# Order of TensorE's work in the attention rounds, and where the recurrence's units stand in it

## The chip, the core and the metric

The kernel runs on one core of a Trainium2 chip. Its engines work side by side, each through its own queue in order: TensorE (PE, with its weight loads as PEld), VectorE (DVE), ScalarE (ACT), GpSimd (POOL), and SyncE (SP), which here only issues transfers. The metric is the device time of one execution in microseconds (us). Everything is computed in fp32.

## What is computed

Four sequences of 1024 tokens with 1024 channels are normalized. An attention layer with 16 query heads and 4 key/value heads of 64 channels, a window of 512 keys and 4 sink keys, makes `s`. A second branch takes the last token of each sequence through a recurrence of four steps, gates with it, normalizes again and makes `g`. The output is `x + s * g`.

```python
mask = (j <= i) & (j >= i - (WINDOW - 1)) | (j < SINK)      # and causal for the first rows
att = softmax(where(mask, q @ k.T / sqrt(HS), -inf))
y = att @ v;  s = y @ Wo.T

thought = x_norm[:, -1, :] @ agg_w + agg_b
for _ in range(4):
    t = layer_norm(thought, pn_gamma, pn_beta)
    t = gelu(t @ d1_w + d1_b)          # 1024 -> 4096
    thought = thought + (t @ d2_w + d2_b)   # 4096 -> 1024
broadcast = thought @ bc_w + bc_b
g = silu(layer_norm(x + sigmoid(x @ gate_w + gate_b) * broadcast))
```

The recurrence works on four rows only. Its weights are read 1 MB at a time: 32 such transfers for d1 and d2, and again in each of the four steps.

## The kernel before

The kernel has three parts. The first makes keys, values, queries and gates (to about 970 us in the profile). The second is attention, with the recurrence between its instructions (to about 1889 us). The third multiplies with `Wo` and writes the output. The change touches the second alone.

Attention runs in 64 rounds, p = 0 to 63 (the loop at L1158). A round has two `Step`s of one pair of query tiles: `far`, a tile with a whole window (tiles 4 to 7 of a sequence), and `near`, a tile of the first half (tiles 0 to 3). A step covers one query tile, one of two key halves `m` and one of two row pairs `rp`, so four rounds belong to a pair of tiles. `n_near`, called n in this text, is the number of key tiles of the near step: 1 for four rounds, then 2, 3, 4, and the same again for each of the four sequences.

The steps' methods, with what each gives to which engine:

- `scores` (L257): TensorE multiplies queries and keys (L277, tiles `S`), VectorE moves the own keys into place (L282), takes the row maximum while it reads the scores (L299, `nm`), and ACT makes the exponentials with their sums (L304). There is a single buffer `S`, of four PSUM banks, for all scores, so scores can start only when the maxima of the scores before them have read it.
- `normalized` (L309): VectorE divides by the sums (L311, L315).
- `turned(k)` (L317): four transposes on TensorE (L322) turn the probabilities of key tile k into a PSUM tile `t`; ACT copies it to SBUF as `pT` (L326). For k = 0 of a far step VectorE also makes `lead` from it (L332).
- `turned_sinks` (L338): the same for the four sink keys, eight matmuls in the 128*32 shape (L344) and ACT's copy `sT` (L349). The tiles `t` and those of the sinks share two PSUM buffers, used in turn.
- `values(k)` (L359): TensorE multiplies `pT` of key tile k with the values (L354) into one tile `y`; `values_apart` (L366) adds the sinks (L371) and `lead`.
- `stored` (L378): VectorE copies `y` out (L384), and POOL's queue stores it (L389).

TensorE's order is written out by hand: the loop is under `manual_schedule` for that engine alone. For all other engines a planner sets the order from the program's order and what it takes to be ready. A round works on the transposes and values of its own steps, and on the scores of the next round's (`far_next`, `near_next`): far scores in two halves, near scores in one.

The recurrence is a generator, `ffn` (L953), that yields after each small unit of work. A stream unit (L977, matmuls at L986) loads 1 MB of weights into one of four buffers and multiplies it, eight matmuls in the 128*32 shape with 512 columns. The last unit of a stream copies the sums to SBUF (L992). The next unit turns them with four transposes (L1040) and adds them up on VectorE. Other units take mean and variance over the 1024 channels (L1060), from which VectorE and POOL make the next step's columns `t_cols` (L1096). The last unit of the first multiplication ends with ACT's gelu (L1107). `filler(slot)` (L1148) stands at three places of a round. It runs as many units as are due at that place, so that all 172 are done by round 62. In the profile a slot holds one unit or none.

Of the kernel before, what the change touches and what calls it, by code (L numbers as in the profile page):

```python
# [44 lines left out]
def recurrent_block_kernel(  # L45
# [356 lines left out]
    def steps_of(tiles, m, rp):  # L402
        return [Step(i, m, rp) for i in tiles]
# [17 lines left out]
    with ExitStack() as a:  # L421
# [434 lines left out]
        with tc.manual_schedule():  # L856
# [4 lines left out]
            for at, (kind, pair) in enumerate(passes):  # L861
                end = at + 1 == len(passes)
                after = None if end else passes[at + 1]
                todo, sums = {}, {}
# [32 lines left out]
                for k, i in enumerate(OUTER):  # L897
# [18 lines left out]
                    if end and k == 3:  # L916
# [9 lines left out]
                        far, near = steps_of(*order[0])  # L926
# [18 lines left out]
    with ExitStack() as a:  # L945
# [7 lines left out]
        def ffn():  # L953
# [23 lines left out]
            def streams(blocks, lhs, name):  # L977

                ps, sums = ps_f.tile([P, WIDE], F32, tag="F", name=f"{name}_ps"), None
                for u, (src, parts) in enumerate(blocks):
                    w = ws.tile([P, 4, WIDE], F32, tag="stream", name=f"{name}_w{u}")
                    nc.sync.dma_start(w, src)
                    for j, (k, moving) in enumerate(parts):
                        nc.tensor.matmul(  # L986
                            ps[j * QUAD : (j + 1) * QUAD, :], lhs[:, k, :], moving(w),
                            start=(u == 0), stop=(u == len(blocks) - 1),
                        )
                    if u == len(blocks) - 1:  # L990
                        sums = px.tile([P, WIDE], F32, tag="wide", name=f"{name}_sb", bufs=1)
                        nc.vector.tensor_copy(sums, ps)  # L992
                    yield sums
# [49 lines left out]
            def add_halves(dst, tr, base):  # L1043

                d4 = dst.rearrange("p (o k) b -> p o k b", o=2)
                b4 = base.rearrange("p (o k) b -> p o k b", o=2)
                nc.vector.tensor_tensor(d4, tr[:, 0:2, :, :B], b4, ALU.add)
                nc.vector.tensor_tensor(d4, tr[:, 2:4, :, :B], d4, ALU.add)
# [19 lines left out]
            def spread(v):  # L1068
                return v.unsqueeze(1).to_broadcast([P, DT, B])
# [8 lines left out]
            base = px.tile([P, DT, B], F32, tag="small", name="base_agg", bufs=4)  # L1078
            nc.vector.tensor_copy(base, along(biases["agg_b"]))
            for sums in streams(wide_blocks(agg_w, 0), t, "agg"):  # L1080
                yield
            add_halves(th, turned_rows(sums, "agg"), base)
            yield

            for s in range(K_STEPS):
                mean = over_d(th, f"mean{s}")
                d = px.tile([P, DT, B], F32, tag="small", name=f"d{s}", bufs=4)
                nc.vector.tensor_tensor(d, th, spread(mean), ALU.subtract)
                sq = px.tile([P, DT, B], F32, tag="small", name=f"sq{s}", bufs=4)
                nc.vector.tensor_mul(sq, d, d)  # L1090
                yield
                var = over_d(sq, f"var{s}")
                r = rstd_of(px, var, P, B, EPS_FFN, f"trs{s}")
                nc.vector.tensor_tensor(d, d, spread(r), ALU.mult)
                nc.vector.tensor_tensor(d, d, along(biases["pn_gamma"]), ALU.mult)
                nc.vector.tensor_tensor(t[:, :, :B], d, along(biases["pn_beta"]), ALU.add)  # L1096
                base = px.tile([P, DT, B], F32, tag="small", name=f"base{s}", bufs=4)
                nc.vector.tensor_tensor(base, th, along(biases["d2_b"]), ALU.add)
                yield
                bias = along_h(biases["d1_b"])  # L1100
                for g in range(H // D):
                    for sums in streams(wide_blocks(d1_w, g), t, f"d1_{s}_{g}"):
                        yield
                    at = slice(g * DT, (g + 1) * DT)
                    add_halves(hid[:, at, :B], turned_rows(sums, f"d1_{s}_{g}"), bias[:, at, :])
                    if g == H // D - 1:
                        nc.scalar.activation(hid[:, :, :B], hid[:, :, :B], AF.Gelu)  # L1107
                    yield
                th = px.tile([P, DT, B], F32, tag="th", name=f"th{s + 1}", bufs=2)
                for o in range(2):  # L1110
                    for sums in streams(deep_blocks(d2_w, o), hid, f"d2_{s}_{o}"):
                        yield
                    at = slice(o * 4, o * 4 + 4)
                    add_quarters(th[:, at, :], turned_rows(sums, f"d2_{s}_{o}"), base[:, at, :])
                    yield

            nc.vector.tensor_copy(t[:, :, :B], th)
            for sums in streams(wide_blocks(bc_w, 0), t, "bc"):
                yield
            ps = ps_f.tile([P, WIDE], F32, tag="F", name="bc_rows_ps")  # L1120
            nc.tensor.matmul(
                ps[: 2 * B, :], sel.rearrange("p b o -> p (b o)"), sums, start=True, stop=True
# [5 lines left out]
        per_half = DT // 2 + 1  # L1128
        FFN_UNITS = 3 + 2 * per_half + K_STEPS * (2 + (H // D) * per_half + 2 * (HT // 4 + 1))

        SLOTS = 3
        ffn_gen, ffn_done, ffn_steps = ffn(), 0, len(order) - 2

        def load_y(n, row):
# [13 lines left out]
        def filler(slot):  # L1148
            nonlocal ffn_done
            due = FFN_UNITS * (p * SLOTS + slot + 1) // (ffn_steps * SLOTS)  # L1150
            while ffn_done < min(due, FFN_UNITS + 1):
                next(ffn_gen, None)
                ffn_done += 1

        with tc.manual_schedule(engines={mybir.EngineType.PE}):
            for p in range(len(order)):  # L1158
                pair, within = divmod(p, per_pair)
                if within == 0:  # L1160
                    b, t = divmod(pair, TT // 2)
                    i = PAIRED[pair][0]
                    own = i % TT
                    leads[i] = px.tile([P, KVD], F32, tag="leads", name=f"leads{i}", bufs=2)
                    nc.vector.tensor_tensor(
                        leads[i], vs[b][:, own - WINDOW // P, :], vs[b][:, own, :], ALU.subtract
                    )
                    if pair + 1 < len(PAIRED):
                        for i in PAIRED[pair + 1]:
                            load_q(i)  # L1170
                    if t == 1 and b + 1 < B:
                        load_kv(b + 1)


                if 0 <= p - 2 * DT < 2 * DT:
                    c, g = divmod(p - 2 * DT, 2)
                    m, r = divmod(c, GROUP)
                    h = (2 * m + g) * GROUP + r
                    tc.keep_in_program_order(
                        nc.sync.dma_start(  # L1180
                            wo_sb[g * HS : (g + 1) * HS, c, :],
                            wo[h // 4, h % 2 * HS : (h % 2 + 1) * HS,
                               h // 2 % 2 * D : (h // 2 % 2 + 1) * D],
                        )
                    )
                if p > 4 * DT:
                    for dst, minuend, subtrahend in islice(wo_parts, 1):
                        tc.keep_in_program_order(
                            nc.vector.tensor_tensor(dst, minuend, subtrahend, ALU.subtract)
                        )  # L1190
                if p == ffn_steps:
                    for _ in ffn_gen:
                        pass
                    for row in range(2):
                        load_y(0, row)
                more = p + 1 < len(order)
                n_near = len(near.keys)
                far.turned(0)
                far.turned_sinks()
                if more:  # L1200
                    far_next, near_next = steps_of(*order[p + 1])
                    far_next.scores((0,))
                for k in (1, 2):
                    far.turned(k)
                filler(0)
                for k in range(3):
                    far.values(k)
                far.turned(3)
                if more:
                    far_next.normalized((0,))  # L1210
                    far_next.scores((1,))
                for k in range(min(2, n_near)):
                    near.turned(k)
                filler(1)
                far.values(3)
                far.values_apart()
                far.stored()
                for k in range(2, n_near):
                    near.turned(k)
                if more:  # L1220
                    far_next.normalized((1,))
                    near_next.scores(both)
                for k in range(n_near):
                    near.values(k)
                if more:
                    near_next.normalized(both)
                near.stored()
                filler(2)
                if more:
                    far, near = far_next, near_next  # L1230

# [275 lines left out]
```

## Time and profile before

| | |
|---|---|
| three timed runs | 2283.7, 2284.26, 2285.59 us (median 2284.26) |
| the profiled execution, its own time | 2284.38 us |
| its span, first to last instruction | 2282.7 us |
| granted TensorE clock, mean | 0.997 |
| score matmuls L277, busy | 259.7 us in 1536 |
| transposes L322, busy | 245.4 us in 1664 |
| values L354, busy | 221.9 us in 1664 |
| copies `pT` L326 on ACT, busy and mean | 229.9 us, 584 ns |
| exponentials L304 on ACT, busy | 324.6 us |

How to read it: a span in the profile is the time from the first to the last instruction. Each engine has a busy time, and groups of instructions are listed by line with the time of one and the idle time of the engine just before them, with what ended that idle time. Matmuls overlap one another in the array, so the busy time of one matmul is longer than the distance to the next; distances between starts tell more. A row of the timeline gives the start in us from the beginning of the span, the time the merged instructions cover, engine, line, operation, what is written and read, the shape, and how many instructions were merged; in brackets stands the idle time of the engine ahead of it and what ended it. ACT has, behind each exponential, a short instruction that reads its sum.

### The profile page before, as it was taken

Reading aid. Unit: us, or ns where it says so; the run is one execution under the profiler, and the core shown is the slowest. Engines: PE = TensorE matmul, PEld = TensorE weight load, DVE = VectorE, ACT = ScalarE, POOL = GpSimd, SP = SyncE. Lnnn points to the kernel's source line nnn. Section 1 sums busy time; section 2 is a strip of 40 time slices with the busy share of each in tenths; the row PEclk is TensorE's granted clock in tenths of the full one; section 3 lists DMA queues with packets and bytes.
Section 4 is the critical chain, followed back from the end, with each engine's and each line's share of the span. In section 5 each row is a group of like instructions: output and inputs, shape, how many; then the busy total and the mean of one; then the engine's idle time right before and its main releaser. Section 6 shows DMA issues by size and latency. Waiting matters only on the chain.

```text
span 2282.7 us, 34177 instructions
## 1 busy us (share of the span) xinstructions
PE 2225.9 (98%) x12614; PEld 1470.9 (64%) x12614; DVE 1735.6 (76%) x3821; ACT 854.5 (37%) x1968; POOL 393.9 (17%) x542
## 2 busy tenths in 40 slices
PE   7899999999999999999999999999999999999999
PEld 6778888888888888855555555555555554444444
DVE  6968688888868788877777777777777776777776
ACT  2121111112100000166665666666656663333332
POOL 3233225425411101310000000100000001111111
PEclk9999999999999999999999999999999999999999
DMA  8695333424533432586667776666566536675653
GB/s 270 233 337 212 107 111 107 147 99 174 215 137 112 160 104 99 163 279 206 192 209 235 229 231 208 210 215 209 169 215 226 190 103 212 179 206 168 171 161 92
DMA packets 214655, 416.60 MB, mean 183 GB/s; under 512 B 13284, under 2 KB 97332, under 8 KB 209368
## 3 DMA queue, kind: packets, MB, share of 16 engines
q1 hardware_dynamic: 170920, 266.12, 36.6%
q0 software_dynamic: 28288, 91.41, 12.9%
q10 hardware_dynamic: 15280, 56.89, 6.8%
q8 instruction: 99, 1.62, 0.3%
q14 instruction: 68, 0.56, 0.1%
HBM read 309.22 MB, written 121.93 MB: 189 GB/s over the span
## 4 chain that ended last, share of the span: by engine, by line
PE 72%; issue 13%; DVE 9%; POOL 3%; DMA 2%; ACT 1%; SPq 0%; POOLq 0%; ACTq 0%; DVEq 0%
PE u L1345 16%; PE u_q L789 13%; PE u_g L789 11%; PE S L277 7%; PE yp L354 7%; PE t L322 7%; PE d_ps L986 4%; PE u L573 3%; DVE t_g L805 2%; DVE st_a L117 1%; DVE f L742 1%; PE yp L371 1%; DVE wq L474 1%; PE xtp L487 1%; ACT pr L304 1%
## 5 line engine op out<-in xcount | busy, mean ns | idle before, releaser
L304 ACT ACTIVATE pr<-pr,nm 128x516 f32<-128x516 f32 (+4 forms) x512 | 324.6, 636 | 154.3 <-DVE nm L299 153.3
L299 DVE CUSTOM_DVE_ANT_0 pr<-S,near_mask 128x516 f32<-128x516 f32 (+4 forms) x512 | 278.3, 589 | 37.7 <-PE S L277 33.3
L326 ACT COPY pT<-t 128x512 f32<-128x512 f32 x416 | 229.9, 584 | 203.5 <-PE t L322 199.2
L277 PE MATMUL S<-kT,qT 64*128 64x512 f32 (+4 forms) x1536 | 259.7, 456 | 2.2 <-DVE nm L299 1.8
L322 PE MATMUL t<-ident,pr 128*128 128x128 f32 x1664 | 245.4, 282 | 7.3 <-ACT pT L326 5.4
L322 PEld LDWEIGHTS t<-ident,pr 128*128 128x128 f32 x1664 | 177.5, 141 | 103.1 <-issue 67.8
L354 PE MATMUL yp<-pT,v 128*64 128x256 f32 x1664 | 221.9, 391 | 0.5 <-DVE y L384 0.4
L277 PEld LDWEIGHTS S<-kT,qT 64*128 64x128 f32 x1536 | 129.6, 186 | 116.8 <-issue 95.5
L789 PE MATMUL u_g<-wg,f 128*128 128x256 f32 x864 | 197.4, 381 | 6.3 <-DVE f L742 6.3
L315 DVE TENSOR_SCALAR pr<-pr,ri 128x516 f32<-128x516 f32 (+4 forms) x512 | 198.6, 435 | 6.1
L789 PE MATMUL u_q<-f,wq_again 128*128 128x256 f32 x896 | 203.1, 379 | 0.0
L354 PEld LDWEIGHTS yp<-pT,v 128*64 128x64 f32 x1664 | 102.2, 136 | 144.3 <-issue 63.6
L789 PEld LDWEIGHTS u_q<-f,wq_again 128*128 128x128 f32 x896 | 169.8, 190 | 24.0 <-DVE f L742 0.9
L789 PEld LDWEIGHTS u_g<-wg,f 128*128 128x128 f32 x864 | 162.8, 190 | 34.0 <-DVE f L742 11.1
L1345 PE MATMUL u<-wo_sb,y 128*128 128x512 f32 x384 | 170.1, 592 | 1.1 <-DVE y L384 1.1
L389 POOL DMA_DIRECT2D y_dram<-y x64 | 36.1, 564 | 751.6 <-DVE y L384 634.4
L311 DVE RECIPROCAL ri<-s 128x2 f32<-128x2 f32 (+1 forms) x192 | 32.8, 171 | 137.3 <-ACT pr L304 136.8
L1345 PEld LDWEIGHTS u<-wo_sb,y 128*128 128x128 f32 x384 | 72.9, 190 | 92.9 <-issue 91.4
L805 DVE TENSOR_TENSOR t_q<-u_q,t_q 128x512 f32<-128x512 f32 x128 | 88.1, 689 | 54.9 <-PE u_q L789 39.3
L805 DVE TENSOR_TENSOR t_g<-u_g,t_g 128x512 f32<-128x512 f32 x128 | 87.9, 686 | 41.2 <-PE u_g L789 36.5
L835 ACT COPY t_q<-u_q 128x512 f32<-128x512 f32 x28 | 16.4, 584 | 273.4 <-PE u_q L789 273.4
L1345 PE MATMUL u<-wo_t,s 128*128 128x512 f32 x256 | 112.5, 592 | 0.0
(262 smaller groups left out, 3591.4 us busy)
## 6 DMA issues: line engine op xcount, KB each, us to landing
d_w<-in_d_w_dram SPq DMA_DIRECT2D x128, 1024.0 KB, 5.7
xT<-xT_dram SPq DMA_DIRECT2D x24, 1024.0 KB, 5.5
xn<-in_x_dram ACTq DMA_DIRECT2D x34, 512.0 KB, 5.1
x<-in_x_dram SPq DMA_DIRECT2D x64, 256.0 KB, 4.6
xT_dram<-xT POOLq DMA_DIRECT2D x32, 512.0 KB, 6.6
qT<-q_dram SPq DMA_DIRECT2D x32, 512.0 KB, 5.3
y_dram<-y POOLq DMA_DIRECT2D x64, 256.0 KB, 3.9
y<-y_dram SPq DMA_DIRECT2D x32, 512.0 KB, 4.7
```

The source lines that it names most:

```text
L277: nc.tensor.matmul(S[:, dst, g, at_s], qTs[self.i][half[g], at + r, :], k, start=True, stop=True,)
L299: nc.vector.tensor_tensor_reduce(out=low, in0=S[:, src, g, :cols], in1=self.mask, scale=-1.0 / HS**0.5, scalar=-NEG, op0=ALU.add, op1=ALU.min,
L304: nc.scalar.activation(low, low, AF.Exp, bias=nm, scale=-1.0, accum_out=self.sums[:, r, g : g + 1],)
L315: nc.vector.tensor_scalar(at, at, rinv[:, r, g : g + 1], None, ALU.mult)
L322: nc.tensor.transpose(ps[:, g, r, :], self.pr[g][:, r, k * P : (k + 1) * P], ident)
L326: nc.scalar.copy(self.pT[k], ps.rearrange("p g r q -> p g (r q)"))
L354: nc.tensor.matmul(self.y[g * HS : (g + 1) * HS, :], v[:, cols], pT[:, g, :], start=first, stop=last,)
L573: nc.tensor.matmul(bank, left[n][i].rearrange("p a (k q) -> p a k q", k=2)[:, c // 2, c % 2, j * P : (j + 1) * P], kv7[i][:, c, :], start= ...
L789: nc.tensor.matmul(bank[:, t * QD : (t + 1) * QD], stationary[:, at : at + P], moving[:, c * QD : (c + 1) * QD], start=(first and c == 0 a ...
L805: nc.vector.tensor_add(dst, in0, in1)
L986: nc.tensor.matmul(ps[j * QUAD : (j + 1) * QUAD, :], lhs[:, k, :], moving(w), start=(u == 0), stop=(u == len(blocks) - 1),)
L1345: nc.tensor.matmul(bank, left[n][i][:, c, j * P : (j + 1) * P], wo7[i][:, c, :], start=(first and c == 0), stop=(c == KH - 1), skip_group_ ...
```

## The change

Five things are changed, all in the attention loop and the generator that fills it.

- The first two transposes of the far step stand together at the start of the round, and the sinks' follow behind slot 0 and not directly behind the first transposes.
- Values come two key tiles at a time, two groups behind their transposes: tiles 0 and 1 behind the next far scores, and tiles 2 and 3 behind the near step's first transposes.
- The third and fourth transposes of the far step stand together, behind the first values.
- The recurrence has two places in a round and not three: slot 0 behind the first two transposes; slot 1 ahead of the second far scores, or, where the near step has one key tile only, at the end of the round. `SLOTS` is 2, so about 1.4 units are due at each place.
- `filler` goes on to a further due unit only if the unit before gave a true value. A stream unit gives one unless it is the last of its stream. All other units give none, and so end the slot; what is due then waits for the next slot.

```diff
-                yield
+                yield sums is None
...
-        SLOTS = 3
+        SLOTS = 2
...
             while ffn_done < min(due, FFN_UNITS + 1):
-                next(ffn_gen, None)
                 ffn_done += 1
+                if not next(ffn_gen, None):
+
+                    break
...
-                far.turned(0)
+                for k in (0, 1):
+                    far.turned(k)
+                filler(0)
                 far.turned_sinks()
                 if more:
                     far_next, near_next = steps_of(*order[p + 1])
                     far_next.scores((0,))
-                for k in (1, 2):
+                for k in (0, 1):
+                    far.values(k)
+                for k in (2, 3):
                     far.turned(k)
-                filler(0)
-                for k in range(3):
-                    far.values(k)
-                far.turned(3)
+                if n_near > 1:
+                    filler(1)
                 if more:
                     far_next.normalized((0,))
                     far_next.scores((1,))
                 for k in range(min(2, n_near)):
                     near.turned(k)
-                filler(1)
-                far.values(3)
+                for k in (2, 3):
+                    far.values(k)
                 far.values_apart()
                 far.stored()
...
                 near.stored()
-                filler(2)
+                if n_near == 1:
+                    filler(1)
```

The first of these hunks stands at four places of the generator, one for each kind of stream. The number of matmuls, transposes, copies and transfers is the same before and after.

## The prediction

> **What bounds the kernel.** I read the page's busy line first, then the stretch from 971 to 1889 us (the attention stage, all that the change touches), then TensorE's waits there, then the timeline of single rounds.
>
> ```profile
> PE 2225.9 (98%) x12614; PEld 1470.9 (64%) x12614; DVE 1735.6 (76%) x3821; ACT 854.5 (37%) x1968; POOL 393.9 (17%) x542
> ...
> 971.00:1889.00 918.00, 905.70 (x7313) 496.69 (x7311) 680.65 (x2202) 576.45 (x1499) 50.62 (x87) 1.00 0.65 207
> ...
> PE t L322 <- ACT pT L326: 5.4, 8, 1.4
> ```
>
> The second line has the stretch, then busy time of PE, PEld, DVE, ACT and POOL, then granted clock and DMA share. TensorE is busy 905.7 of 918 us and ACT 576 of 918. The third line is TensorE's longest wait there: 5.4 us in eight cases, for the copy of a transposed tile. So TensorE bounds the stage, and only two things can move the time: how densely its instructions follow each other, and new waits. Density shows in the starts of its groups, here a round with n = 4 near key tiles:
>
> ```profile
> 1396.49 1.99 PE L277 MATMUL S<-kT,qT 64*128 64x512 f32 x8
> 1398.41 1.95 PE L354 MATMUL yp<-pT,v 128*64 128x256 f32 x16
> 1400.28 1.07 PE L986 MATMUL d_ps<-d_w,hid_cols 128*32 128x512 f32 x8
> 1401.28 0.66 PE L322 MATMUL t<-ident,pr 128*128 128x128 f32 x4
> 1401.87 0.42 PE L344 MATMUL st<-ident,pr 128*32 128x128 f32 x8
> 1402.22 1.35 PE L277 MATMUL S<-kT,qT 64*128 64x512 f32 x8
> 1403.51 1.09 PE L322 MATMUL t<-ident,pr 128*128 128x128 f32 x8
> 1404.53 1.06 PE L986 MATMUL d_ps<-d_w,hid_cols 128*32 128x512 f32 x8
> 1405.53 1.52 PE L354 MATMUL yp<-pT,v 128*64 128x256 f32 x12
> 1406.97 0.66 PE L322 MATMUL t<-ident,pr 128*128 128x128 f32 x4
> 1407.56 1.35 PE L277 MATMUL S<-kT,qT 64*128 64x512 f32 x8
> ```
>
> From start to start, four transposes take 0.59 us (1406.97 to 1407.56) and eight take 1.02 (1403.51 to 1404.53): four more cost 0.43, so 0.16 belongs to the group, not to its work. Twelve value matmuls take 1.44 and sixteen 1.87: again 0.43 more, 0.15 per group. A stream unit takes 1.00; at the 0.11 of 128 columns, its two sets of 512 are 0.87, which leaves 0.13.
>
> **What goes.** The first two transposes of a round stand together: one group less in each of 64 rounds, 64 x 0.155 = 9.9 us. Before, 136 stream units and 64 sink groups (both 128*32) stood apart: 200 groups. The generator has 172 units. Only a stream unit that is not the last of its stream returns true, and a slot ends at the first unit that doesn't; with due = 173(2p + slot + 1)/124, rounded down, I counted the units slot by slot. In 47 rounds stream units stand in slot 0, directly ahead of the sinks, and 41 further groups stand in slot 1: 105 groups instead of 200, 95 x 0.13 = 12.4. Together **-22.3 us**. The values two groups behind their transposes change no count.
>
> That stream units and sinks merge without a price rests on their common shape. The Trainium skill, TensorEngine Tiling (Array Packing), Key Properties, says that changing the tiling mode, not the tile, drains the array. By that rule the 47 seams are free. The trace has a seam inside one mode: an output transpose of the recurrence behind a round's transposes, both 128*128, costs 0.06 over its columns; that would make 2.8 us. I take 0, since matmuls of 256, 128 and 256 columns in one value group show no seam, and keep 2.8 for the range.
>
> **What comes: the sinks wait for ACT.** Transposes and sinks share two PSUM buffers. Before, the third tile of a round was asked for behind the scores; now the sinks ask for it, behind the first two transposes and slot 0. They need the first copy of the round, and ACT makes that copy behind the near step's exponentials:
>
> ```profile
> 1401.39 0.71 ACT L304 ACTIVATE pr<-pr,nm 128x512 f32<-128x512 f32 x1
> ...
> 1402.09 0.56 ACT L326 COPY pT<-t 128x512 f32<-128x512 f32 x1
> ...
> 1828.88 0.60 PE L322 MATMUL t<-ident,pr 128*128 128x128 f32 x4
> ...
> 1829.92 0.71 ACT L304 ACTIVATE pr<-pr,nm 128x512 f32<-128x512 f32 x1
> 1830.63 0.56 ACT L326 COPY pT<-t 128x512 f32<-128x512 f32 x1
> ```
>
> The last three lines are the case that decides the order: with no unit between values and transposes, the transposes were over at 1829.5, and yet the fourth exponential went first, at 1829.92. TensorE went on 0.61 us after that copy's start (the next transposes began at 1831.24).
>
> Now the timetable for n = 4, from the near scores' start: copy starts at 5.60 (1402.09 - 1396.49), so sinks may start at 6.21. Values end at 3.79, eight transposes make it 4.81. An empty slot 0 waits 1.40; four output transposes (0.50) leave 0.90; one stream unit (0.87) leaves 0.54; two leave nothing. The same from rounds with fewer near tiles: n = 3: 1.26, 0.76, 0.40; n = 2: 1.14, 0.64, 0.28; n = 1 is mostly covered, since slot 1 stands behind its values. In the first round of a pair the near step is one tile larger than the values that cover it; there n = 3 waits 0.84 and n = 4 0.97 with one unit. By the slot count: n = 1 gives 1.6 us, n = 2 five rounds of 0.64 and five of 0.28 (4.6), n = 3 4.0, n = 4 9.9. **+20.0 us** in 31 rounds. Bounds: 0, if the copy goes ahead of the exponentials; 25, if near exponentials of n = 1 and 2 come 0.2 to 0.5 later, because 0.57 less work lies between second scores and near scores (a stream unit out, four values in). I take 20.
>
> **Transposes behind copies.** With n = 1, slot 1 no longer lies between the third and fourth transposes and the scores. The near transposes need the third copy. Counted from the first scores' end: maxima at 1.2 and 1.9, exponentials 1.31 to 2.84, copy from 2.84, TensorE free for it at 3.45; TensorE arrives at 1.02 + 1.02 + 1.29 = 3.31. 0.14 x 16 = 2.2, and some 1.5 in rounds whose slot 1 holds next to nothing. **+3.7**, between 0 (the copy ahead of the second exponential) and 9 (one more copy of 0.56 ahead, sixteen times).
>
> **The recurrence.** Held-back units wait less only where the next slot is far. In n = 1, slot 1 of a round and slot 0 of the next are only eight transposes apart, and in rounds 3 and 17 the variance falls there, with the first stream unit of the step behind it. Nearest rows:
>
> ```profile
> 1223.43 1.94 PE L986 MATMUL d_ps<-d_w,t_cols 128*32 128x512 f32 x8 [2.29 <-DVE t_cols L1096]
> 1225.29 1.12 PE L322 MATMUL t<-ident,pr 128*128 128x128 f32 x4
> ...
> 1223.40:1227.00 3.60, 3.57 (x22) 1.37 (x24) 1.78 (x10) 1.67 (x8) 0.60 (x1) 0.57 0.33 85
> ...
> 1431.30 0.41 PE L1060 MATMUL var_ps<-sq,ones 128*128 128x32 f32 x2
> ...
> 1435.22 1.06 PE L986 MATMUL d_ps<-d_w,t_cols 128*32 128x512 f32 x8 [0.38 <-DVE t_cols L1096]
> ```
>
> Variance to stream took 3.92 in the later case. Now 0.24 + 1.02 lies between: 2.7 us of waiting. The first rows show what such a wait does: after 2.29 us idle the granted clock was 0.57 over 3.6 us, the stream unit took 1.86 instead of 1.00 and the transposes 1.05 instead of 0.59, 1.3 us more. The Trainium skill, TensorE: Matmul & The Clock Gate, What's actually happening, gives the half clock after at least one idle window of about 3.4 us. By that rule two waits of 2.7 cost 5.4; by the row 8.0. I take the row. Gone are the old ones: 3.6 at 1223 (2.29 + 0.86 + 0.46) and 0.38 at 1435. **+4.0** (from -2.4, if only five VectorE operations of 0.17 to 0.19 and POOL's power of 1.12 stand in the chain, to +6.7, with the 5.3 us from the variance at 1218.10 to 1223.43).
>
> Gelu's two table loads (1.28 each) fall mid-round as before: 0, from -2 to +3. Old waits for a copy at the third transposes, 0.9 in all, become part of the sinks' wait: -0.9. Weights have four buffers and no burst uses one again within 10 us, against 5.7 us to land: 0.
>
> **Sum.** -22.3 + 20.0 + 3.7 + 4.0 - 0.9 = +4.5, upon 2284.4 (the profiled run; its span is 2282.7, and the median of three is 2284.3, so it stands for them): **2289 us**. A measurement can tell 0.2%, 4.6 us, from no change, so this forecast lies at the edge of slower.
>
> **Rivals.**
> First (62%), as summed: groups saved, given back at the sinks; 2279 to 2299 by the bounds above. Of it, 5 faster, 22 within, 35 slower.
> Second (17%), the gain stands: the planner puts the first copy ahead of the last exponentials, or the exponentials end earlier. Then the 20.0 fall out: 2269. It decides the other side as soon as the copies start 1 us earlier. For it: ACT has 340 us to spare in the stage. Against: the exponentials went first even where both were ready.
> Third (21%), slower by more: the second scores, which stand only 2.0 us behind the first, wait for the maxima to leave the single score buffer. With n = 4 and empty slots this was seen at 1868.06 (0.83 us waited). If a VectorE copy of 0.68 comes ahead of the maxima in the 16 rounds of n = 1 and some ten with a thin slot 1, 26 x 0.6 = 15: 2304. It decides from one such copy in each round on; against it, VectorE is busy only 681 of 918 us.
>
> The range 2267 to 2303 leaves out part of the second and half of the third. Faster 22%, same 22%, slower 56%.
>
> **What would show it.** Line 344 (sinks) idle some 20 us for ACT's copy in about 31 rounds, mostly n = 3 and 4, with fewer than two units ahead; a wait of 2 to 4 us with half clock in rounds 3/4 and 17/18; about 745 groups instead of 904. The prediction is wrong if the sinks don't wait, or if score matmuls do in most rounds.

## The result, and the profile after

The changed kernel takes 2302.06 us (median of six, 2299.62 to 2302.95) against 2283.95 us of the kernel before (six, 2283.09 to 2285.59). The ratio is 1.0076, with a 95% interval of 1.0065 to 1.0087. It is slower by 18 us; forecast were 2289 us and slower.

First the page's busy line of the changed kernel, then its attention stage (in the window view: the stretch, its length, busy time of PE, PEld, DVE, ACT and POOL, granted clock, DMA share), then TensorE's longest waits there:

```profile
PE 2212.0 (96%) x12614; PEld 1481.3 (64%) x12614; DVE 1735.8 (75%) x3821; ACT 850.9 (37%) x1968; POOL 397.1 (17%) x542
```
```profile
971.00:1905.20 934.20, 894.86 (x7327) 509.08 (x7328) 681.79 (x2202) 572.60 (x1500) 52.31 (x88) 0.99 0.61 204
```
```profile
PE st L344 <- ACT pT L326: 22.6, 31, 3.2
PE d_ps L986 <- issue: 7.4, 2, 3.9
PE d_ps L986 <- PE t L322: 3.1, 4, 0.8
PE S L277 <- DVE th L1052: 1.5, 2, 1.1
```

The stage is 16 us longer, 934 instead of 918, which is the whole difference of the two spans (2299.2 and 2282.7). TensorE does the same work in it with 11 us less busy time, and yet its share fell: the array is better packed, and stands still longer. The first row of the waits was not there before. Thirty-one times the sinks' matmuls waited for ACT's copy of a transposed tile: once at the start of the stage (3.2 us), and thirty times in later rounds.

To see both sides in one measure I took the starts of all groups of TensorE's work in the two traces, and took off each group's columns at the distances that the prediction read from the timeline. What is left is a fixed price per group and waits. The count starts with the near scores at about 962 us, so that its stretch is 927 us long before the change:

| us | before | after |
|---|---|---|
| groups from 962 us on | 904 | 745 |
| fixed price of the groups | 139.1 | 117.0 |
| waits | 23.6 | 62.1 |
| of these, the sinks for ACT's copy, from round 1 on | 0 | 24.8 |
| recurrence behind the end of an n = 1 round, and its half clock | 4.2 | 15.9 |
| gelu | 2.4 | 1.8 |
| start of the stage | 9.1 | 12.2 |
| other | 7.9 | 7.4 |

22.1 us were saved, and 38.5 came in as waits. Two places hold nearly all of them. Here is the first, a round with four near tiles and one stream unit in slot 0 (TensorE, then ACT):

```profile
1155.74 1.99 PE L277 MATMUL S<-kT,qT 64*128 64x512 f32 x8
1157.65 1.95 PE L354 MATMUL yp<-pT,v 128*64 128x256 f32 x16
1159.53 1.09 PE L322 MATMUL t<-ident,pr 128*128 128x128 f32 x8
1160.55 1.06 PE L986 MATMUL d_ps<-d_w,hid_cols 128*32 128x512 f32 x8
1161.96 0.43 PE L344 MATMUL st<-ident,pr 128*32 128x128 f32 x8 [0.34 <-ACT pT L326]
1162.31 1.35 PE L277 MATMUL S<-kT,qT 64*128 64x512 f32 x8
```
```profile
1159.93 0.71 ACT L304 ACTIVATE pr<-pr,nm 128x512 f32<-128x512 f32 x1
...
1160.64 0.70 ACT L304 ACTIVATE pr<-pr,nm 128x512 f32<-128x512 f32 x1
...
1161.34 1.04 ACT L326 COPY pT<-t 128x512 f32<-128x512 f32 x2
```

The copy starts 5.60 us after the near scores (1161.34 - 1155.74) and the sinks 6.22 after them. The timetable had 5.60 and 6.21. A stream unit takes 0.87 when it merges with the sinks, so without the wait they had stood at 1161.42: 0.54 late, of which the bracket shows the 0.34 in which the modelled ends of the matmuls had passed too. The last near exponential, at 1160.64, is what the copy stands behind.

The second place, rounds 17 and 18 (TensorE, then the window view of what follows):

```profile
1230.45 0.41 PE L1060 MATMUL var_ps<-sq,ones 128*128 128x32 f32 x2
1230.69 1.20 PE L322 MATMUL t<-ident,pr 128*128 128x128 f32 x8
1235.41 3.59 PE L986 MATMUL d_ps<-d_w,t_cols 128*32 128x512 f32 x16 [3.52 <-issue]
1238.79 0.43 PE L344 MATMUL st<-ident,pr 128*32 128x128 f32 x8
```
```profile
1235.40:1238.80 3.40, 3.39 (x17) 0.91 (x21) 0.00 (x0) 0.00 (x0) 0.00 (x0) 0.50 0.12 14
```

From the variance to the stream unit it takes 4.96 us, and only eight transposes lie between. Then the granted clock is 0.50, and two stream units take 3.38 us instead of 1.74. Rounds 3 and 4 show the same; both together lost 11.0 us.

### The profile page after: what moved, and what is told of

The parts are those of the page before. It is cut to its first block, busy times and chain, and to the rows that moved or that the text cites. A ratio compares the mean times of both kernels' runs of the same rounds, so it can differ in the third digit from the quotient of the medians.

```text
span 2299.2 us, 34231 instructions
## 1 busy us (share of the span) xinstructions
PE 2212.0 (96%) x12614; PEld 1481.3 (64%) x12614; DVE 1735.8 (75%) x3821; ACT 850.9 (37%) x1968; POOL 397.1 (17%) x542
## 4 chain that ended last, share of the span: by engine, by line
PE 69%; issue 14%; DVE 10%; POOL 3%; ACT 2%; DMA 2%; POOLq 0%; ACTq 0%; SPq 0%; DVEq 0%
PE u L1350 16%; PE u_q L789 13%; PE u_g L789 11%; PE S L277 7%; PE yp L354 6%; PE t L322 6%; PE d_ps L986 4%; PE u L573 3%; DVE t_g L805 2%; ACT pr L304 1%; DVE st_a L117 1%; DVE f L742 1%; PE yp L371 1%; DVE wq L474 1%; PE xtp L487 1%
## 5 line engine op out<-in xcount | busy, mean ns | idle before, releaser
L326 ACT COPY pT<-t 128x512 f32<-128x512 f32 x416 | 223.6, 579 | 126.2 <-PE t L322 118.3
L322 PE MATMUL t<-ident,pr 128*128 128x128 f32 x1664 | 231.4, 280 | 3.0 <-DVE t_q L805 1.4
L835 ACT COPY t_q<-u_q 128x512 f32<-128x512 f32 x28 | 16.4, 585 | 273.3 <-PE u_q L789 273.3
```

The lines of the kernel that those rows point to most:

```text
L322: nc.tensor.transpose(ps[:, g, r, :], self.pr[g][:, r, k * P : (k + 1) * P], ident)
L326: nc.scalar.copy(self.pT[k], ps.rearrange("p g r q -> p g (r q)"))
```

## The experiments

The theory after the result: (1) the sinks wait for ACT's first copy, because nothing but slot 0 covers the near exponentials that stand ahead of it; (2) the end of an n = 1 round is too near to the next slot 0. The main rival: ACT and VectorE are late as a whole, and a wait taken away at one place comes back at the next.

Behind each time stand its ratio to the kernel before, run beside it (2284.8 to 2286.5 us in these runs), and the 95% interval of the ratio.

### More of the suspected wait, and less of it

`sinks_first` takes the cover away: sinks ahead of slot 0.

```diff
-                filler(0)
                 far.turned_sinks()
+                filler(0)
```

> The changed kernel with the sinks ahead of slot 0, so that nothing but eight transposes covers ACT's exponentials. Theory (timetable of the prediction with an empty slot 0 in every round: 1.14, 1.26 and 1.40 us for n = 2, 3, 4 and the 0.2 to 0.3 us that the runs showed beyond it): the sinks wait 60 to 70 us in all, and the time is about 2342 us. Rival (the wait comes of the stream units ahead of the sinks): no more than now, about 2302 us.

2355.95 us, ratio 1.0305 (1.0289 to 1.032). Its waits:

```profile
PE st L344 <- ACT pT L326: 84.2, 64, 3.2
PE d_ps L986 <- DVE t_cols L1096: 3.0, 2, 1.5
```

The wait is now in every round, 1.2 to 1.8 us in most, near the 1.14 to 1.40 of an uncovered slot. The sum is larger than forecast (84 against 60 to 70), since rounds with one near tile wait 0.3 to 1.5 us too, a pair's first round up to 1.9, and rounds behind a gelu 2.5. What decides is how much work of TensorE stands between near scores and sinks. Stream units do not cause the wait; they shorten it.

`scores_first` puts 1.29 us of scores ahead of slot 0 and the sinks.

```diff
-                filler(0)
-                far.turned_sinks()
                 if more:
                     far_next, near_next = steps_of(*order[p + 1])
                     far_next.scores((0,))
+                filler(0)
+                far.turned_sinks()
```

> The changed kernel with one edit: the next far step's first scores stand ahead of slot 0 and the sinks. Theory (the sinks wait for ACT's first copy, for lack of 1.29 us of work ahead of them): the sinks' wait falls from 22.6 us to under 3 us, the waits of n = 1 rounds behind slot 1 lose 1.3 us each, and the time goes from 2302 to about 2272 us. Rival (the wait only moves, because ACT and VectorE are late as a whole): the first values or the second scores wait instead, and the time stays above 2295 us.

2299.51 us, ratio 1.006 (1.0045 to 1.0075). The rival's number came, and the waits show why:

```profile
PE t L322 <- ACT sT L349: 9.9, 13, 1.1
PE S L277 <- DVE nm L299: 8.3, 16, 1.5
PE d_ps L986 <- issue: 4.7, 2, 2.4
...
PE st L344 <- ACT pT L326: 3.3, 2, 1.9
```

The sinks' wait is gone as forecast: of 3.3 us, most lies at the start of the stage. In its place the far step's fourth transposes wait for the sinks' copy `sT`, since they get the sinks' buffer. One case, in rows of ACT and TensorE:

```profile
1260.53 0.73 ACT L304 ACTIVATE pr<-pr,nm 128x516 f32<-128x516 f32 x1 [2.15 <-DVE nm L299]
...
1261.26 0.71 ACT L304 ACTIVATE pr<-pr,nm 128x516 f32<-128x516 f32 x1
1261.97 0.24 ACT L349 COPY sT<-st 128x128 f32<-128x128 f32 x1
...
1262.26 0.66 PE L322 MATMUL t<-ident,pr 128*128 128x128 f32 x4 [0.47 <-ACT sT L349]
```

The sinks' copy now stands behind both exponentials of the first scores, as the first copy had stood behind those of the near scores. And the second scores wait for the maxima, since fewer groups lie between the two scores. The waits behind the n = 1 rounds did get shorter (the longest of them 2.4 us, not 3.9), but slot 0 now stands one group of scores nearer to slot 1, and the recurrence waits there, 2.9 us at a gelu among others. So theory (1) names the wait rightly, but the two PSUM buffers and the one score buffer pass it on. A third buffer for the tiles, the most direct test of that, was not tried.

### The end of the n = 1 rounds

`slot1_mid` calls `filler(1)` ahead of the second scores in all rounds.

```diff
-                if n_near > 1:
-                    filler(1)
+                filler(1)
...
-                if n_near == 1:
-                    filler(1)
```

> The changed kernel with one edit: slot 1 stands ahead of the second far scores in rounds of one near tile too, and not at their end. Theory (17 to 18 us are lost where slot 1 at the end of a round is followed by slot 0 of the next, eight transposes later): stream, mean and output units there no longer wait, both stretches of half clock go, about -17 us; the sinks of these rounds lose a unit of cover, +8 to +12 us; about 2294 us. Rival (the recurrence's chain costs what it costs, wherever its units stand): within 3 us of 2302.

2295.0 us, ratio 1.0042 (1.0028 to 1.0056): the theory's number. No half clock is left between the stage's start and its end, and the sinks of n = 1 rounds pay for the cover that they lost:

```profile
PE st L344 <- ACT pT L326: 29.6, 40, 3.2
```

`both`, the two edits together, was to show whether they add up.

> Both edits together: scores ahead of slot 0 and the sinks, slot 1 ahead of the second scores in all rounds. Theory: both groups of waits go and the saved groups remain, about 2262 us, some 22 us under the kernel before. Rival (waits move on to the second scores, the near transposes or the values): 2280 us or more.

They do not: 2308.64 us, ratio 1.0097 (1.0082 to 1.0113). In n = 1 rounds slot 1 no longer lies between the last values and the next transposes, and the passed-on waits grow: transposes for `sT` 12.0 us, scores for the maxima 11.5.

### The copy on another engine

`copy_dve` changes only which engine makes the first copy of a far step.

```diff
-            nc.scalar.copy(self.pT[k], ps.rearrange("p g r q -> p g (r q)"))
+            copy = nc.vector.tensor_copy if self.far and k == 0 else nc.scalar.copy
+            copy(self.pT[k], ps.rearrange("p g r q -> p g (r q)"))
```

> The changed kernel with one edit: the copy of a far step's first transposed tile is made by VectorE, not by ACT. Theory (the sinks wait for that one copy because it stands behind the near exponentials on ACT): VectorE ends the near maxima earlier than ACT its exponentials, so the copy ends about 0.5 us earlier, and the sinks' wait falls from 22.6 us to about 9; about 2288 us. Rival (moved work lengthens VectorE's chain, and the second scores or the normalized rows wait for it): the sinks' wait falls, but score and transpose matmuls wait as much more; 2300 us or over.

2298.48 us, ratio 1.0059 (1.0044 to 1.0074), 10 us over the forecast. The sinks' wait fell nearly as expected, to 11.2 us in the last two of these rows. But the recurrence's stream units at the head of a round wait longer (the lines of this kernel are one higher):

```profile
PE d_ps L987 <- issue: 13.6, 6, 4.1
PE st L345 <- ACT pT L327: 7.9, 8, 3.2
PE st L345 <- DVE pT L327: 3.3, 8, 0.7
```

VectorE's copy now stands ahead of the small operations from which `t_cols` and the sums come, just where theory (2) says there is no room: six units of the recurrence, in rounds 3, 17, 34, 36, 50 and 52, wait 0.6 to 0.7 us longer each, about the length of the copy (0.68).

The second row holds the start of the stage (3.2 us) and seven waits in rounds 37 to 46 that are as long as in the changed kernel. In these seven VectorE has an operation of 0.68 us on `Wo` (L1192) directly ahead of the copy, so that the copy ends no earlier than it did on ACT, and nothing is gained. Elsewhere the longer waits fell by 0.6 to 0.8 us.

`copy_dve_mid` has slot 1 in the middle as well (the diff of `slot1_mid`), and so tells whether that is the reason.

> The same, and slot 1 stands ahead of the second far scores in all rounds. Theory: the sinks' wait goes from 29.6 us (slot 1 in the middle, copy on ACT) to about 12, and the waits behind the rounds' ends stay away: about 2279 us, some 5 us under the kernel before. Rival: as above, 2293 us or over.

2280.78 us, ratio 0.9983 (0.9976 to 0.999), as forecast. The sinks' wait fell from 29.6 to 14.7 us. With slot 1 in the middle, moving this one copy off ACT brings 14 us (2295.0 to 2280.8); with slot 1 at the end only 4. That supports both theories at once: the copy's place behind the exponentials is the cause of the sinks' wait, and the end of the n = 1 rounds has no room.

### Holding units back

`no_hold` runs all due units of a slot.

```diff
                 ffn_done += 1
-                if not next(ffn_gen, None):
-
-                    break
+                next(ffn_gen, None)
```

> The changed kernel without the break: a slot runs all units that are due. Theory (held-back units save waits): 19 pairs of dependent units stand next to each other in a slot, and sums, means, variance and gelu are waited for there, 10 to 20 us; about 2315 us. Rival (holding back costs more than it saves, since it pushes units to the ends of n = 1 rounds): 2302 us or less.

2317.13 us, ratio 1.014 (1.0124 to 1.0155). Without holding back, the output transposes wait 6.7 us for the sums' copy, and means, variances and gelu as forecast. This part of the change is worth 15 us where slots hold more than one unit.

### The new generator with the old order

`old_order` leaves transposes and values as they were before, and takes from the change the generator, two slots, and slot 0 in front of the sinks. Against the kernel before:

```diff
                 far.turned(0)
+                filler(0)
                 far.turned_sinks()
...
                 for k in (1, 2):
                     far.turned(k)
-                filler(0)
...
                 near.stored()
-                filler(2)
```

> The kernel before, with the new generator alone: two slots, units that wait held back, slot 0 between the first transposes and the sinks, slot 1 where it was (ahead of the last far values), nothing at the end of the round. All transposes and values stand as before, so that the third tile of a round is again asked for behind the first scores. Theory (the merged stream units are a gain, and the loss comes of the sinks being the third to ask for a buffer): 95 groups fewer than before, 12 us gained, under 4 us of waits added; about 2274 us. Rival (two slots make the recurrence or ACT late as such): 2284 us or over.

2275.64 us, ratio 0.9958 (0.9943 to 0.9973). Here the sinks are again the second to ask for a buffer, and the third, a transpose, stands behind the first scores:

```profile
PE S L277 <- DVE nm L299: 6.9, 11, 0.9
PE t L322 <- ACT pT L326: 3.7, 6, 1.4
```

The merged groups are kept, and the sinks do not appear among the waits. What is new is the first row: the stream unit that stood between the two far scores is gone.

`two_slots` asked which part of that is the gain. It keeps slots 0 and 1 where they were and drops slot 2, so that stream units and sinks stay apart.

```diff
                 near.stored()
-                filler(2)
```

> The kernel before with the new generator alone, and its slots 0 and 1 where they were (behind the second and third transposes, and ahead of the last far values); slot 2 is gone. Stream units and sinks stay apart. Theory: 136 stream units in 88 groups, 48 groups fewer, -6.2 us; one old wait for the recurrence's columns less, -4; the third tile of a round is asked for without a unit ahead of it, +3 to +4 us for ACT's copy in rounds with 3 and 4 near tiles; about 2278 us. Rival (it is the seam between stream units and sinks that brings the whole gain): 2283 us or more.

2293.16 us, ratio 1.0036 (1.0022 to 1.005): not the theory's number, and the wrong side of the kernel before. It lies in the rival's range, but the seam alone does not explain a loss. The waits tell why:

```profile
PE t L322 <- ACT pT L326: 10.7, 24, 1.5
PE S L277 <- DVE nm L299: 7.5, 15, 1.6
```

Slot 2 had been the cover of the near exponentials and maxima. Without it, transposes wait for the copy 24 times, and scores, mostly the first of a round, for the maxima: together 11 us more than in the kernel before (18.2 against 7.2), where I had given 3 to 4. One of these waits, 1.63 us at 1017.6, is followed by half clock. In `old_order` slot 0, moved ahead of the sinks, is that cover. It does two things at once: it merges with the sinks, and it stands where the old slot 2 stood for the purpose of ACT.

`old_order_mid` moves slot 1 of `old_order` ahead of the second scores, to take away the 6.9 us.

```diff
                 far.turned(3)
+                filler(1)
...
                 for k in range(min(2, n_near)):
                     near.turned(k)
-                filler(1)
```

> The kernel with the old order of transposes and values, the new generator, and slot 0 ahead of the sinks, with one more edit: slot 1 stands ahead of the second far scores. Theory (score matmuls there wait 6.9 us for the maxima, because the stream unit that stood between the two scores is gone, and 3 us are lost where the variance is followed by a stream unit): both go, about 2267 us. Rival (the near scores or the near exponentials come late in their place): 2274 us or more.

2277.38 us, ratio 0.9966 (0.9954 to 0.9978). The rival is right. The waits for the maxima fall to 4.1 us and move to the near scores. Nothing lies any longer between the second scores and the near ones of n = 1 rounds but transposes and values: there the next round's first transposes are held up by 0.4 to 0.5 us for their normalized rows in eleven rounds. In two rounds the near scores wait 1.8 us, behind the recurrence's variance on VectorE, and one of these two waits is followed by half clock. So the last one, `old_order_four`, does it with four near tiles only.

```diff
                 far.turned(3)
+                if n_near == 4:
+                    filler(1)
...
-                filler(1)
+                if n_near < 4:
+                    filler(1)
```

> The kernel with the old order of transposes and values, the new generator, and slot 0 ahead of the sinks; slot 1 stands ahead of the second far scores only in rounds of four near tiles, and ahead of the last far values in all others. Theory (the second scores' wait for the maxima, some 6 us, comes in rounds of four near tiles, and slot 1 ahead of them does harm only with one near tile): about 2270 us. Rival (it costs as much at the near scores): 2275 us or more.

2270.89 us, ratio 0.9936 (0.9922 to 0.9949): below both kernels. Its stage and its waits:

```profile
971.00:1874.00 903.00, 892.37 (x7310) 500.56 (x7310) 680.38 (x2201) 573.39 (x1499) 51.03 (x87) 1.00 0.63 211
```
```profile
PE t L322 <- ACT pT L326: 3.7, 6, 1.4
PE S L277 <- DVE nm L299: 3.1, 6, 0.8
```

TensorE is busy 892 us, nearly as in the changed kernel (895), in a stage that is 31 us shorter. ACT and VectorE are as busy as there (573 and 680 us; 573 and 682), so neither was late as a whole: the order made the waits.

## Why the prediction was right, and where its sizes were off

- **The number.** Forecast were 4.5 us more, measured 18.1. The 2302 us lie within the range of 2267 to 2303, but 3 us above the 2279 to 2299 that the summed path was given. What reached beyond 2299 was the third rival, and its cause did not come. The side and the two largest terms were right by their mechanism; that the range held is in part luck.
- **What bounds the stage.** Right: only packing and waits moved the time. Busy time fell by 11 us and the stage grew by 16.
- **What goes, -22.3.** Measured -22.1. The groups are 745, and the seam between stream units and sinks costs next to nothing: what a stream unit takes beyond its columns is at most 0.02 ahead of the sinks, against 0.13 ahead of values. The rule that only a changed mode drains the array (the Trainium skill, TensorEngine Tiling (Array Packing), Key Properties) agrees with that. The 0.06 at the output transposes was no price on top: the next group pays 0.10 behind them instead of 0.155, so that together it is the price of one group.
- **Sinks, +20.0.** Mechanism, place and number of waits as forecast (31; measured 30). The size is 24.8, at the upper bound that was given. The cases that the timetable gives for three and four near tiles are met to 0.04 us; one more round, behind a gelu, waits 0.8. With two near tiles the last exponential ends 3.90 us after the near scores' start and not 3.63. The reason named for the bound fits: the second scores stand nearer to the near ones, and in the trace VectorE is still dividing their rows when the near scores are ready. That makes 3 us in ten rounds.
- **Transposes behind copies, +3.7.** Nearly nothing came at that place: near transposes waited 0.7 us over a whole stage. (The sum has a slip, too: 1.02 + 1.02 + 1.29 is 3.33 and not 3.31, which makes 1.9 of the 2.2.) Second scores waited some 4 us in single rounds (2 us before), but the kernel before had waited some 3 us for copies in others, so the term should have been about 0.
- **The recurrence, +4.0.** This is the term that was most mis-sized: +11.7, beyond its own upper bound of +6.7. The two variance waits were 11.0 us and not 8.0, since from variance to stream unit it took 4.96 us at round 17 and 5.22 at round 3, not the 3.92 of the row that I took. The difference lies at the head of the chain, on VectorE, where the variance is summed up (first before the change, then after it):

```profile
1431.84 0.16 DVE L1065 TENSOR_REDUCE var<-var_ps 128x4 f32<-128x32 f32 x1
...
1232.16 0.18 DVE L1065 TENSOR_REDUCE var<-var_ps 128x4 f32<-128x32 f32 x1
```

In the row that I took, it starts 0.54 us behind the variance's matmul (1431.30). At round 17 it starts 1.71 us behind it (1230.45), because VectorE first divides the second far rows, takes the four near maxima and copies `y`. From there on the two chains are alike, 3.38 and 3.25 us. The longest chain that the prediction knew, 5.3 us, would have covered it. And six more units wait at the same place, in rounds 3, 17, 34, 36, 50 and 52: a mean or a first stream unit stands eight transposes behind the output transposes of the unit before, and waits 0.7 to 0.9 us each for VectorE's sums, 4.9 us in all. The prediction had named the place and then asked only what the variance would do there; it had given the other held-back units no price. In `slot1_mid` these waits are gone but for some 0.4 us.
- **The clock.** Idle stretches of 3.5 and 3.9 us were each followed by 3.41 us at 0.50, 1.6 us lost each (1.3 forecast). That does not decide between the row and the rule of an idle window of about 3.4 us (the Trainium skill, TensorE: Matmul & The Clock Gate, What's actually happening), since both stretches are longer than that. Other runs show that the length of the stretch alone does not decide: in `two_slots` the half clock came behind 1.63 us of idle time, and in `scores_first` it did not come behind 2.39 us (at 1022.15, granted clock 1.00).
- **The start of the stage** was not in the sum: its first sinks waited 3.2 us for their copy, and half clock followed (0.50 from 972.6 to 976.0); with both, the start took about 3 us more than before.
- **Rivals.** The second did not come: in no round of the trace did the copy go ahead of the near exponentials. The third, second scores waiting for the maxima, is not what made this kernel slower, but it is what came up in `scores_first` and `old_order` when less work lay between the two scores.

The sum with the measured terms, -22.1 + 24.8 + 11.7 + 3 - 0.6 (gelu) and nothing for the rest, is 16.8, beside 16.4 by the starts of the groups and 16.5 in the spans. The timed runs differ by 18.1. The other 1.6 us are the choice of the executions: the profiled one of the changed kernel took 2300.9 us, 1.2 under the median, and that of the kernel before 2284.4, 0.4 over it.

## What to carry to other kernels

Work that looks like filling between two groups is also the cover of some other engine's queue; before it is moved or merged, ask which copy or exponential it had been hiding, and work out the new distance from the instruction that starts that queue's work. A ring of two buffers turns any reordering into a question of who asks third, and ahead of what. And where a generator's units are held back to the next slot, every pair of neighbouring slots must be far enough apart for the longest chain between two units, not only on the average.

## What the runs showed of the hardware

- A group of matmuls of one shape pays a fixed price when the shape changes: 0.13 to 0.20 us here, 139 us of the 927 us from 962 to 1889 in the kernel before. A change in the number of columns within one shape pays next to nothing (stream units of 512 and sinks of 128 columns: at most 0.02).
- An idle stretch of TensorE can cost half as much again as it lasts: idle for 3.52 us at 1231.9, the granted clock was 0.50 for the next 3.4 us, and 1.6 us were lost. Idle for 2.29 us, in the kernel before, did the same, and so did 1.63 us in `two_slots`. The length alone does not settle it: 2.39 us in `scores_first` did not, nor did the waits of 1.2 to 1.8 us in most rounds of `sinks_first`.
